# Row numbers of a feed-forward's dequantization constants: from VectorE in the first layer's attention to GpSimd at the front, and the pieces behind them one step earlier

## The chip, the core and the metric

The kernel runs on one core of one Trainium2 chip. The metric is the device time of one execution in microseconds (us). Before the change it is 2844.29 us, the median of three runs (2843.87 to 2844.41).

Engines are named as in the profile: PE is the TensorE matrix engine and PEld its weight load, DVE is VectorE, ACT is ScalarE, POOL is GpSimd, and SP is the engine whose queue issues most of the DMAs. L190 stands for line 190 of the kernel before.

## The reference

Two transformer layers run one after the other on 2048 tokens of width 512 (32 sequences of 64). Each layer is a cross-attention with 32 query heads and 8 key heads, followed by a feed-forward part. The second layer's feed-forward is a small memory lookup, which the change does not touch. The first layer's feed-forward has weights of 4 bits, which are unpacked with a scale and a zero for every group of 128 rows:

```python
x = x + _L0_xattn_ref(_layernorm(x), ctx_4096, ctx_4096, mask1, wq, wk, wv, wo)
x = x + _L0_ffn_ref(_layernorm(x), qweight_gu, qzeros_gu, scales_gu, g_idx_gu,
                    qweight_down, qzeros_down, scales_down, g_idx_down)
x = x + _L1_xattn_ref(_layernorm(x), ctx_4096, mask0, q_w, k_w, v_w, o_w, q_norm, k_norm)
x = x + _L1_ffn_ref(_layernorm(x), ...)

def _L0_ffn_ref(x, qweight_gu, qzeros_gu, scales_gu, g_idx_gu, ...):
    def _dequant(qw, qz, sc, g_idx):
        wq = (qw[:, None, :] >> shifts & 15)          # 4-bit weights
        zq = (qz[:, :, None] >> shifts & 15) + 1.0    # 4-bit zeros, one per group and column
        return sc[g_idx] * (wq - zq[g_idx])           # a row's group picks its scale and zero
    gate, up = split(x @ _dequant(gu))                # 512 -> 2 x 1376
    return (silu(gate) * up) @ _dequant(down)         # 1376 -> 512
```

## The kernel before

**Tiling.** The 2048 tokens are four chunks of 512. Attention runs over eight key heads g, each with its four query heads, and over the four chunks c: 32 steps (g, c), which this text numbers 4g + c, from step 0 to step 31. Each large product is cut into 2 x 2 blocks and made of seven block products where eight would be usual (`quarters` and `output_first`/`output_rest`); for that POOL adds and subtracts blocks of the operands (`left_sums`, `right_sums`).

**One step of the first layer's attention** (`Attention.run`, L672). While DVE, ACT and POOL work on the softmax of step i, PE finishes the output product of the step before (`output_rest`), projects the keys of step i+1 (`pk`, L375), projects its queries (`P`, L189, seven block products), multiplies probabilities and values (`po`, L609), projects the next values (`pv`, L407), begins the output product of step i (`O`, L189) and takes the next scores (`S`, L508). So the first `pk` of a step marks one step's beginning on PE, and the distance from one to the next is the length of a step. In a query projection ACT copies a block product out of PSUM (`h`, L214), DVE adds the next one to it (L439), ACT and DVE turn it by its position (`rotate`, L422 to L425) and POOL adds the two halves (L426). Keys are turned the same way (`rk`). In steps with c = 0 and g > 0, POOL has four more operations in this stretch, the `right_sums` of the output weights `wo` (L174 to L177), and in steps with c = 3 the `left_sums` of the next query weights.

**The order of the work.** The program is written as a list. A scheduler at build time orders the instructions of each engine: the order of the text is the priority, but an instruction that is ready in its model while earlier ones are not may be put ahead of them. `tc.issue_after(ins)` holds the instructions of a block on `ins`'s engine behind `ins`. On the chip each engine, and each DMA queue, then works strictly in that fixed order. Buffers of one tag go round: `tmp` has two of 128 x 1024 values (every `rotate` takes one), `m2` has four of 128 x 512 (the softmax takes two per step).

**The constants** (`ffn_constants`, L775) are made in pieces by a generator. In `att0.run` the argument `late` (L1350) takes one piece in each of the 24 steps 4 to 27, behind the last output addition on DVE (L709 to L711). The pieces are, in this order:

- one piece: the row numbers `pidx` (L781 to L795). Each of four ranges of partitions gets a counter from POOL (`iota`), and then DVE makes of it two flags, -1 where the counter has reached one or two times the number of groups, and takes that number off where a flag is set. That leaves group numbers in column 0 and the flags in columns 1 and 2.
- seven pieces: the scales, 512 columns at a time (L798 to L814). Three DMAs bring the columns into a `tmp` buffer, and five DVE operations split them into three bf16 parts, with the flags as a scalar operand.
- eight pieces: the zeros (L815 to L833). Two DMAs bring them into an `m2` buffer; each piece unpacks two of eight nibbles with four DVE operations.
- eight pieces: the group numbers (L834 to L856). One DMA each, and four DVE operations that compare with column 0 of `pidx`.

They are used from step 30 on, by the matmuls L922 and L940.

**The front.** Four DMAs on ACT's queue bring the first chunk of x. DVE takes its statistics (`norm_stats`, L258 to L262), POOL makes the reciprocal root (`rsqrt`, L247), DVE scales (L272), PE transposes (L286), ACT copies back (L290), and POOL makes the `right_sums` of the result. Before that POOL sets a few small constants (L117 to L147).

Of the kernel before, what the change touches and what calls it, by code (L numbers as in the profile page):

```python
# [9 lines left out]
F32 = mybir.dt.float32  # L10
BF16 = mybir.dt.bfloat16
# [4 lines left out]
ALU = mybir.AluOpType  # L16
AX = mybir.AxisListType

P = 128
# [14 lines left out]
INTER = 1376  # L34
# [10 lines left out]
def tile_xattn_ffn_2_layers(ctx: ExitStack, tc: tile.TileContext, a: dict, out: bass.AP):  # L45
    nc = tc.nc
# [5 lines left out]
    const = ctx.enter_context(tc.tile_pool(name="const", bufs=1))  # L52
# [12 lines left out]
    def m2_tile(name):  # L65
        return ap_.tile([P, CH], F32, tag="m2", name=name, bufs=4)
# [19 lines left out]
    def tmp_tile(name):  # L86
        return ap_.tile([P, 2, CH], F32, tag="tmp", name=name)
# [157 lines left out]
    def rsqrt(dst, src):  # L245

        return nc.gpsimd.tensor_tensor(dst, src, nhalf[:, : src.shape[-1]], ALU.pow).ins  # L247
# [3 lines left out]
    def norm_stats(c, name, at_once=TT):  # L251

        st = sm.tile([P, TT, 6], F32, tag="st", name=f"st{name}{c}")
        mv = sm.tile([P, TT, 2], F32, tag="mv", name=f"mv{name}{c}")
        ve = sm.tile([P, TT], F32, tag="ve", name=f"ve{name}{c}")
        rs = sm.tile([P, TT], F32, tag="rs", name=f"rs{name}{c}")
        for t in range(TT):
            nc.vector.bn_stats(st[:, t, :], x_sb[c][:, t, :])  # L258
            nc.vector.bn_aggr(mv[:, t, :], st[:, t, :])
            if (t + 1) % at_once == 0:  # L260
                part = slice(t + 1 - at_once, t + 1)
                nc.vector.tensor_scalar(ve[:, part], mv[:, part, 1], EPS, None, ALU.add)  # L262
                rsqrt(rs[:, part], ve[:, part])
        norms[c] = mv, rs
# [36 lines left out]
    def norm_apply(c, name):  # L301
        norm_scale(c, name)
        return norm_turn(c, name)
# [468 lines left out]
    NG, NGD = a["scales_gu"].shape[0], a["scales_down"].shape[0]  # L772
    ffn = {}

    def ffn_constants():  # L775


        both = const.tile([P, 3 * INTER], BF16, tag="c8", name="szoh")
        sz, oh = both[:, 0 : 2 * INTER], both[:, 2 * INTER :]
        pidx = const.tile([P, 3], F32, tag="pidx", name="pidx")  # L780
        for base, cnt, parts in ((R_GS, NG, 3), (R_GZ, NG, 1), (R_DS, NGD, 3), (R_DZ, NGD, 1)):  # L781
            rows = slice(base, base + parts * cnt)
            idx, p1, p2 = (pidx[rows, k : k + 1] for k in range(3))
            nc.gpsimd.iota(
                idx,
                pattern=[[0, 1]],
                base=0,
                channel_multiplier=1,
                allow_small_or_imprecise_dtypes=True,
            )  # L790

            nc.vector.tensor_scalar(p1, idx, float(cnt), -1.0, ALU.is_ge, ALU.mult)
            nc.vector.tensor_scalar(p2, idx, float(2 * cnt), -1.0, ALU.is_ge, ALU.mult)
            for p_ in (p1, p2):
                nc.vector.scalar_tensor_tensor(idx, p_, float(cnt), idx, ALU.mult, ALU.add)  # L795
        ffn["sz"], ffn["oh"] = sz, oh
        yield
        for base, cnt, name in ((R_GS, NG, "scales_gu"), (R_DS, NGD, "scales_down")):  # L798
            rows = slice(base, base + 3 * cnt)
            _, p1, p2 = (pidx[rows, k : k + 1] for k in range(3))  # L800
            total = a[name].shape[1]
            for at in range(0, total, CH):
                w = min(CH, total - at)
                s = tmp_tile(f"{name}{at}")
                v, part = s[rows, 0, 0:w], s[:, 1, :].bitcast(BF16)[rows, 0:w]
                for k in range(3):
                    nc.sync.dma_start(
                        s[base + k * cnt : base + (k + 1) * cnt, 0, 0:w], a[name][:, at : at + w]
                    )
                for by in (p1, p2):  # L810
                    nc.vector.tensor_copy(part, v)
                    nc.vector.scalar_tensor_tensor(v, part, by, v, ALU.mult, ALU.add)
                nc.vector.tensor_copy(sz[rows, at : at + w], v)
                yield  # L814
        qz = m2_tile("qz").bitcast(U32)  # L815
        zi = m2_tile("zi").bitcast(U32)
        for base, cnt, name in ((R_GZ, NG, "qzeros_gu"), (R_DZ, NGD, "qzeros_down")):
            w = a[name].shape[1]
            rows = slice(base, base + cnt)
            nc.sync.dma_start(qz[rows, 0:w], a[name])  # L820
            zv = sz[rows, 0 : 8 * w].rearrange("p (w e) -> p w e", e=8)
            for e in range(8):
                nc.vector.tensor_scalar(
                    zi[rows, 0:w],
                    qz[rows, 0:w],
                    4 * e,
                    15,
                    ALU.logical_shift_right,
                    ALU.bitwise_and,
                )  # L830
                nc.vector.tensor_copy(zv[:, :, e], zi[rows, 0:w])
                if e % 2 == 1:
                    yield  # L833
        for base, cnt, parts, name in (  # L834
            (R_GS, NG, 3, "g_idx_gu"),
            (R_GZ, NG, 1, "g_idx_gu"),
            (R_DS, NGD, 3, "g_idx_down"),
            (R_DZ, NGD, 1, "g_idx_down"),
        ):
            rows = slice(base, base + parts * cnt)  # L840
            total = a[name].shape[1]
            for at in range(0, total, CH):
                w = min(CH, total - at)
                gt = tmp_tile(f"{name}{base}_{at}")
                gv, o = gt[rows, 0, 0:w].bitcast(I32), gt[rows, 1, 0:w]
                nc.sync.dma_start(
                    gv, a[name][0:1, at : at + w].to_broadcast([parts * cnt, w])
                )

                nc.vector.tensor_scalar(o, gv, 0.0, float(cnt), ALU.is_lt, ALU.mult)  # L850
                nc.vector.tensor_tensor(o, o, gv, ALU.add)
                nc.vector.tensor_scalar(o, o, 0.0, float(cnt - 1), ALU.max, ALU.min)
                nc.vector.tensor_scalar(
                    oh[rows, at : at + w], o, pidx[rows, 0:1], None, ALU.is_equal
                )
                yield  # L856
# [457 lines left out]
    nc.sync.dma_start(wqk[:, 0:1], a["q_norm"])  # L1314
    nc.sync.dma_start(wqk[:, 1:2], a["k_norm"])

    norm_stats(0, "a")
    first = norm_apply(0, "a")
    att0.start()

    def behind_first(c):
        with tc.issue_after(first):
# [3 lines left out]
            if c < last:  # L1326
                load_mask(c + 1)
                norm_stats(c + 1, "a")
                norm_apply(c + 1, "a")

    pieces = ffn_constants()
    first_up = []

# [149 lines left out]
```

## Time and profile before

| what | us |
|---|---|
| median of the runs | 2844.29 |
| the profiled execution, its own time | 2844.26 |
| its span in the profile | 2842.5 |
| PE busy in the span | 2796.1 |
| DVE, POOL and ACT busy | 1874.9, 1322.1 and 835.1 |
| length of most steps of the first attention | 35.38 |
| step 4 (row numbers, c = 0) | 37.93 |
| step 8 (fifth piece of scales, c = 0) | 36.68 |
| step 12 (first piece of zeros, c = 0) | 37.32 |
| steps 16, 20 and 24 (c = 0) | 35.38, 36.16 and 35.94 |

The execution's own time is 1.8 us longer than its span, which runs from the first to the last instruction. Lengths of steps are distances between the starts of the first `pk` matmuls (190.67 and 228.60 us for step 4, for instance). In lines of the timeline the columns are: start and duration in us, engine, line, operation, output <- input, shapes and count (several like instructions in a row are merged into one line), and in brackets the idle time before with what ended it.

### The profile page before, as it was taken

To read this page: it belongs to the slowest core of one execution; us is meant where nothing else is said; L and a number is where in the kernel's file an instruction comes from. 1 tells how busy PE (TensorE), PEld (TensorE's weight loads), DVE (VectorE), ACT (ScalarE), POOL (GpSimd) and SP (SyncE) were. 2 spreads that over 40 slices of the span, in tenths; PEclk is the share of its full clock that TensorE was granted. 3 is DMA by queue.
4 is the path that set the end of the run, shared out by engine and by line. 5 is a ranking of instruction groups with operands and counts; after the bars stand their busy time and mean duration, and the time that the engine had idled before them with its cause. 6 is when DMAs were issued, how large, how long until landed. Compare 5 with 4: busy or idle time off the path is not lost. (4 is left out here: it accounts for less than half of the span.)

```text
span 2842.5 us, 41235 instructions
## 1 busy us (share of the span) xinstructions
PE 2796.1 (98%) x16742; PEld 2259.8 (80%) x16742; DVE 1874.9 (66%) x2805; ACT 835.1 (29%) x1415; POOL 1322.1 (47%) x1039
## 2 busy tenths in 40 slices
PE   7999999999999999999999999999999999999998
PEld 5878787888888887888888677888888888888775
DVE  7777777777777777756655665555555555555667
ACT  3333333333333333311111322222222222222244
POOL 5554545454545455644443444444444444444332
PEclk9999999999999999999999999999999999999999
DMA  4111111111111110100001102111111111111001
GB/s 165 34 52 45 54 42 57 36 62 38 60 39 61 38 60 16 53 23 23 23 6 37 48 30 62 43 53 45 53 45 53 45 52 45 53 45 53 30 1 60
DMA packets 103812, 130.77 MB, mean 46 GB/s; under 512 B 8725, under 2 KB 65165, under 8 KB 103623
## 3 DMA queue, kind: packets, MB, share of 16 engines
q1 hardware_dynamic: 103047, 127.09, 13.8%
q8 instruction: 133, 2.18, 0.3%
q10 hardware_dynamic: 576, 1.05, 0.1%
q14 instruction: 56, 0.46, 0.1%
HBM read 123.92 MB, written 4.19 MB: 45 GB/s over the span
## 5 line engine op out<-in xcount | busy, mean ns | idle before, releaser
L189 PE MATMUL O<-wo,oT 128*128 128x256 f32 x3584 | 802.3, 381 | 0.6 <-DVE x L242 0.5
L189 PE MATMUL P<-xnT,wq 128*128 128x256 f32 x3584 | 789.4, 380 | 10.6 <-ACT h L214 10.5
L189 PEld LDWEIGHTS P<-xnT,wq 128*128 128x128 f32 x3584 | 682.1, 191 | 133.7 <-issue 35.1
L189 PEld LDWEIGHTS O<-wo,oT 128*128 128x128 f32 x3584 | 670.3, 190 | 114.3 <-issue 24.6
L242 DVE TENSOR_TENSOR x<-x,O 128x512 f32<-128x512 f32 (+1 forms) x448 | 368.6, 823 | 235.7 <-PE O L189 235.5
L589 POOL TENSOR_TENSOR s<-s,ib 128x512 f32<-128x512 f32 x128 | 169.4, 1343 | 518.4 <-DVE ib L313 471.8
L214 ACT COPY h<-P 128x512 f32<-128x512 f32 (+1 forms) x352 | 202.4, 575 | 561.0 <-PE P L189 559.3
L247 POOL TENSOR_TENSOR qr<-qs,nhalf 128x20 f32<-128x20 f32 x32 | 113.4, 3543 | 382.7 <-DVE qs L496 382.7
L426 POOL TENSOR_TENSOR qT<-h,rq 128x512 f32<-128x512 f32 x128 | 175.4, 1370 | 237.6 <-DVE rq L425 237.6
L583 ACT ACTIVATE s<-s 128x1024 f32<-128x1024 f32 x64 | 67.7, 1057 | 735.9 <-DVE s L581 735.9
L189 PE MATMUL P<-xnT,wgu 128*128 128x256 f32 (+1 forms) x1232 | 271.3, 380 | 0.4 <-DVE x L242 0.2
L189 PEld LDWEIGHTS P<-xnT,wgu 128*128 128x128 f32 (+1 forms) x1232 | 229.8, 187 | 40.2 <-DVE x L242 4.3
L407 PE MATMUL pv<-wkv,ctxT 128*128 128x128 f32 x1984 | 246.2, 280 | 1.6 <-DVE h L439 1.6
L407 PEld LDWEIGHTS pv<-wkv,ctxT 128*128 128x128 f32 x1984 | 228.5, 192 | 23.0 <-issue 18.2
L375 PE MATMUL pk<-ctxT,wkv 128*128 128x512 f32 x496 | 223.2, 593 | 0.3 <-DVE h L439 0.3
L422 ACT COPY rq<-h 64x512 f32<-64x512 f32 x256 | 157.9, 617 | 124.1 <-DVE h L439 119.1
L424 DVE TENSOR_TENSOR h<-h,cosT 128x512 f32<-128x512 f32 x128 | 92.7, 724 | 123.8 <-ACT rq L422 123.6
L375 PEld LDWEIGHTS pk<-ctxT,wkv 128*128 128x128 f32 x496 | 94.1, 190 | 93.5 <-issue 89.6
L457 DVE TENSOR_TENSOR qT<-h,P 128x512 f32<-128x512 f32 x128 | 87.7, 686 | 100.8 <-PE P L189 94.3
L463 DVE TRANSPOSE_TENSOR_REDUCE part<-q 128x16 f32<-128x512 f32 x128 | 90.8, 709 | 87.6 <-ACT q L459 83.8
L965 DVE TENSOR_TENSOR h<-h,P 128x512 f32<-128x512 f32 (+1 forms) x96 | 61.1, 640 | 127.7 <-PE P L189 95.0
L972 POOL TENSOR_TENSOR hT<-h,h 128x512 f32<-128x512 f32 (+1 forms) x48 | 56.5, 1181 | 187.4 <-DVE h L965 187.4
(250 smaller groups left out, 3418.9 us busy)
## 6 DMA issues: line engine op xcount, KB each, us to landing
ctxT<-in_ctxT SPq DMA_DIRECT2D x62, 1024.0 KB
wq<-in_L_wq SPq DMA_DIRECT2D x32, 256.0 KB
wo<-in_L_wo SPq DMA_DIRECT2D x32, 256.0 KB
wq<-in_L_wqT SPq DMA_DIRECT2D x32, 256.0 KB
wo<-in_L_woT SPq DMA_DIRECT2D x32, 256.0 KB
wgu<-in_qweight_gu SPq DMA_DIRECT2D x40, 128.0 KB
out<-o SPq DMA_DIRECT2D x16, 256.0 KB
x<-in_x SPq DMA_DIRECT2D x12, 256.0 KB
```

Source lines behind the costliest of these rows:

```text
L189: ins = nc.tensor.matmul(pv[0:w, m, :], left[:, l, k, m * P : m * P + w], right[:, r, k, :], start=(first and m == 0 and k == 0), stop=(k ...
L214: last_copy = nc.scalar.copy(t[size], ps[size]).ins
L242: return nc.vector.tensor_tensor(dst, dst, src, ALU.add).ins
L247: return nc.gpsimd.tensor_tensor(dst, src, nhalf[:, : src.shape[-1]], ALU.pow).ins
L375: nc.tensor.matmul(ps, wkv[:, k, 0, :], ctxT[:, k, :], start=(k == 0), stop=(k == KT - 1))
L407: nc.tensor.matmul(ps[:, t * HD : (t + 1) * HD], ctxT[:, k, t * P : (t + 1) * P], wkv[:, k, 1, :], start=(k == 0), stop=(k == KT - 1),)
L422: nc.scalar.copy(t[lo:hi, 1], src[HD - hi : HD - lo])
L424: nc.vector.tensor_tensor(view(x), view(src), over(cosT), ALU.mult)
L426: nc.gpsimd.tensor_tensor(dst(None), dst(x), dst(t[:, 1]), ALU.add)
L457: nc.vector.tensor_tensor(q, xv, yv, ALU.add)
L463: nc.vector.tensor_reduce(part[:, i, f], q2.rearrange("p (g q) -> p g q", q=KB), AX.X, ALU.add, apply_transpose=True,)
L589: nc.gpsimd.tensor_tensor(sv[:, f], sv[:, f], ib[:, f * W : (f + 1) * W].unsqueeze(1).to_broadcast([P, KH, W]), ALU.mult,)
```

## The change

- The `iota`s and the arithmetic on `pidx` leave the generator. A new function `ffn_indices` does them, called at the front right ahead of `norm_stats(0, "a")`.
- The arithmetic goes from DVE to POOL. [...]
- The arithmetic is made for two of the four ranges only, those with three parts; the other two keep their counter. So 16 operations on DVE become 12 on POOL: eight `tensor_scalar` and four `tensor_tensor`. The four `iota`s stay.
- The generator loses its first `yield`. So the first piece of scales runs where the row numbers ran (step 4), each later piece runs one step sooner, and step 27 has none.

```diff
-    def ffn_constants():
-        both = const.tile([P, 3 * INTER], BF16, tag="c8", name="szoh")
-        sz, oh = both[:, 0 : 2 * INTER], both[:, 2 * INTER :]
-        pidx = const.tile([P, 3], F32, tag="pidx", name="pidx")
+    pidx = const.tile([P, 4], F32, tag="pidx", name="pidx")
+
+    def ffn_indices():
         for base, cnt, parts in ((R_GS, NG, 3), (R_GZ, NG, 1), (R_DS, NGD, 3), (R_DZ, NGD, 1)):
             rows = slice(base, base + parts * cnt)
             idx, p1, p2 = (pidx[rows, k : k + 1] for k in range(3))
             nc.gpsimd.iota(idx, ...)
-            nc.vector.tensor_scalar(p1, idx, float(cnt), -1.0, ALU.is_ge, ALU.mult)
-            nc.vector.tensor_scalar(p2, idx, float(2 * cnt), -1.0, ALU.is_ge, ALU.mult)
+            if parts == 1:
+                continue
+            tt, ts = nc.gpsimd.tensor_tensor, nc.gpsimd.tensor_scalar
+            ts(p1, idx, float(cnt), -1.0, ALU.is_ge, ALU.mult)
+            ts(p2, idx, float(2 * cnt), -1.0, ALU.is_ge, ALU.mult)
+            x = pidx[rows, 3:4]
             for p_ in (p1, p2):
-                nc.vector.scalar_tensor_tensor(idx, p_, float(cnt), idx, ALU.mult, ALU.add)
+                ts(x, p_, float(cnt), None, ALU.mult)
+                tt(idx, idx, x, ALU.add)
+
+    def ffn_constants():
+        both = const.tile([P, 3 * INTER], BF16, tag="c8", name="szoh")
+        sz, oh = both[:, 0 : 2 * INTER], both[:, 2 * INTER :]
         ffn["sz"], ffn["oh"] = sz, oh
-        yield
         for base, cnt, name in ((R_GS, NG, "scales_gu"), (R_DS, NGD, "scales_down")):
...
+    ffn_indices()
     norm_stats(0, "a")
     first = norm_apply(0, "a")
     att0.start()
```

## The prediction, made before the changed kernel was run

> **What bounds the kernel now.** I read the busy times first, then the waits of PE, then the lengths of the steps, then the step and the front that the change touches. PE is the bound:
>
> ```profile
> PE 2796.1 (98%) x16742; PEld 2259.8 (80%) x16742; DVE 1874.9 (66%) x2805; ACT 835.1 (29%) x1415; POOL 1322.1 (47%) x1039
> ```
>
> It is not busy for 2842.5 - 2796.1 = 46.4 us, so work on DVE or POOL counts only where it makes PE wait. The view of PE's waits (who waited for whom: total us, times, longest us) says where:
>
> ```profile
> PE xta L286 <- DVE xna L272: 12.0, 2, 11.8
> PE P L189 <- ACT h L214: 10.5, 7, 3.2
> ...
> PE pv L407 <- DVE h L439: 1.6, 4, 0.6
> ```
>
> 11.8 us is the start, before the first transpose. The second and fourth lines are query projections in which DVE is late with the addition L439: a block buffer comes free late, ACT copies late, PE waits. PE's timeline gives the place of one of them, and the lengths of steps:
>
> ```profile
> 190.67 3.60 PE L375 MATMUL pk<-ctxT,wkv 128*128 128x512 f32 x8
> 205.19 3.72 PE L189 MATMUL P<-xnT,wq 128*128 128x256 f32 x16 [2.29 <-ACT h L214]
> 228.60 3.60 PE L375 MATMUL pk<-ctxT,wkv 128*128 128x512 f32 x8
> 263.98 3.60 PE L375 MATMUL pk<-ctxT,wkv 128*128 128x512 f32 x8
> ```
>
> 263.98 - 228.60 = 35.38 us is an undisturbed step, 228.60 - 190.67 = 37.93 is step 4. All steps from 4 to 27 are 35.38 except 4 (+2.55), 8 (+1.30), 11 (+0.11), 12 (+1.94), 20 (+0.78) and 24 (+0.56): 7.24 us is all that pieces of constants can cost now. Five of the six have c = 0, where POOL also makes the sums of `wo`. Step 4's timeline on DVE and POOL shows why:
>
> ```profile
> 193.51 0.10 DVE L795 SCALAR_TENSOR_TENSOR pidx<-pidx 12x1 f32<-12x1 f32 x1
> ...
> 193.75 2.49 POOL L589 TENSOR_TENSOR s<-s,ib 128x512 f32<-128x512 f32 x2 [10.71 <-DVE pidx L795]
> 193.88 1.15 DVE L795 SCALAR_TENSOR_TENSOR pidx<-pidx 12x1 f32<-12x1 f32 x1
> ...
> 197.88 3.40 DVE L795 SCALAR_TENSOR_TENSOR pidx<-pidx 30x1 f32<-30x1 f32 x3
> ...
> 202.51 0.68 DVE L439 TENSOR_TENSOR h<-h,P 128x512 f32<-128x512 f32 x1
> ```
>
> A dozen values take 0.10 us while POOL is idle and 1.15 while it runs a large addition: DVE waits for POOL's operation to end, and each short instruction pays that anew. The 16 operations hold DVE from 192.75 to 201.28, so L439 comes 202.51 - 190.67 = 11.84 us into the step. Taking PE's resumption minus its wait in steps 4, 8 and 12 (14.52 - 2.29, 12.65 - 0.43, 13.90 - 1.67) gives 12.22 to 12.23 each time, so L439 has until about 11.84 - 2.29 = 9.6 us.
>
> The Trainium skill, page "GPSIMD Engine Reference", its opening table: GpSimd's SBUF interfaces are shared with VectorE, with contention for VectorE instructions that have two SBUF inputs or run in a two-port mode. The pair 0.10 and 1.15 agrees.
>
> **Step 4: row numbers out, scales in.** Out go 16 DVE operations, in come the five of a scales piece (two casts, two multiply-adds, one last cast). The same piece at the same kind of step is step 8's: there its operations stand between 336.81 and 342.90, and the keys' L424 starts 342.83 - 334.74 = 8.09 us into the step; in step 4 it starts 201.31 - 190.67 = 10.64. I take step 8's length whole: 36.68 - 37.93 = **-1.25**. Bounds: -2.55 (nothing left) and 0 (POOL's order holds DVE as long). Still late there is step 8's own remainder, 0.43 on `P` and 0.30 on `pv`. Its three DMAs go ahead of a load of ctx and the four of `wo` on SP's queue; in step 8 these are issued at 320.12, 321.12 and 334.93, the last held by PE and not by the three, which cost SP 0.95 us. The buffer they need comes free at the last turned query of the step before, as there. So 0 for the DMAs; without the 14 us between, a `wo` would land 1 us later.
>
> **Step 12: zeros, first piece out, second in.** Now DVE waits 0.54 us for the zeros' DMA (issued at 478.84 between loads of `wo`), the piece runs from 481.33 to 487.44 through POOL's sums, and L439 comes 11.23 us in. The second piece has no DMA. In step 13 it ends 521.73 - 514.99 = 6.74 us in, with its reciprocal (L586) at 1.33; with c = 0 that stands at 1.91 (step 8), so the piece ends near 7.3. L424 at 6.36 (step 20) went with a length of 36.16, at 8.09 (step 8) with 36.68; on that line 7.3 gives 36.44: **-0.88**. Bounds: -1.94 and 0. The wait for the DMA moves to step 11, c = 3, in which no `wo` is loaded and SP's queue is free after 429.7 + 0.5 until 463.7. There L439 stands at 9.46 behind the scales of 5.05 us (444.93 to 449.98), and the zeros take about as long: 0, at most +0.5.
>
> **The other pieces.** Step 16 gets the second pair of a set for the first, like for like (both 0.19, 0.31, 1.12 and 1.31 us): 0. Step 20 gets 4 x 512 for 12 x 512 (800.74 to 805.43 against 764.71 to 769.07, 0.33 longer), step 24 gets 10 x 512 for 30 x 352 (942.80 to 947.52 against 907.12 to 911.40, 0.44 longer). By the slope of the two steps above (0.52 per 1.73 us) that is +0.10 and +0.13, or +0.22 for step 24 if it becomes step 20: together **+0.3**, bounds 0 and +0.6. Step 8 keeps a piece of the same shape: 0. All steps with c = 1 to 3 but step 11 are 35.38 with pieces of each kind, cover included: 0. Step 27 loses a piece that cost nothing. `tmp` and `m2` are taken as often as before, one step sooner; the constants are used 100 us later.
>
> **The front.** POOL gets four `iota`s and twelve small operations ahead of the `rsqrt` that starts the whole chain; behind it wait the scaling, the transposes and PE.
>
> ```profile
> 9.81 0.17 DVE L262 TENSOR_SCALAR vea<-mva 128x4 f32<-128x4 f32 x1
> ...
> 10.14 1.07 POOL L247 TENSOR_TENSOR rsa<-vea,nhalf 128x4 f32<-128x4 f32 x1 [8.60 <-DVE vea L262]
> ...
> 11.18 1.09 POOL L784 IOTA pidx<- 12x1 f32 x4
> ```
>
> POOL is idle for 8.60 us there, from 1.54. No row shows these operations on one column; nearest are groups of 128 x 4 (busy us, mean ns):
>
> ```profile
> L1126 POOL TENSOR_SCALAR up<-rsd 128x4 f32<-128x4 f32 x4 | 2.1, 533 | 0.3
> L1127 POOL TENSOR_TENSOR up<-mvd,rsd 128x4 f32<-128x4 f32 x4 | 1.4, 354 | 0.0
> L1128 POOL TENSOR_SCALAR up<-up 128x4 f32<-128x4 f32 x4 | 1.4, 352 | 0.3
> L1265 POOL TENSOR_SCALAR g_ub<-g_lv,g_rec 128x4 f32<-128x4 f32 x1 | 0.7, 725 | 0.0
> L1267 POOL TENSOR_SCALAR g_ub<-g_ub 128x4 f32<-128x4 f32 x1 | 0.7, 674 | 0.7 <-DVE g_ub L1266 0.7
> ```
>
> Back to back the first three take 1.04 us together (2679.59 to 2680.63), 0.35 each; the five from L1267 to L1271 take 2.41 (2832.74 to 2835.15), 0.48 each. 1.54 + 1.09 + 12 x 0.48 = 8.4 us, 1.7 before POOL is needed: **0**. With the longest, 0.725, it is 11.3: +1.2. With the farthest row, the 1.03 us of a `rsqrt` of 128 x 4, 15.0: +4.9. No gain is possible: the chain waits for x until 8.87. What is late on this chain passes to PE whole, which has no gap from the transposes to `P` at 22.73. On DVE an early POOL operation could hold a statistic by one small operation; idle time of 0.5 to 0.9 us ahead of each covers that.
>
> The Trainium skill, same page, section "Elementwise — side-by-side cycle accounting", speaks against the move: elementwise work belongs on VectorE while GpSimd's software is as it is. By that each operation should be dearer on POOL, and 0.35 against 0.10 agrees; it changes nothing while the 8.60 us cover it.
>
> **Sum.** -1.25 - 0.88 + 0.3 + 0 = -1.8 us. On the profiled execution: span 2840.7, own time 2842.4; that run was 0.03 below the median, so **2842.5**. The bounds add to -4.5 (-2.55 - 1.94) and +2.3 (0.6 + 0.5 + 1.2), for 2839.8 and 2846.6.
>
> **Rivals.** 0.2% or 5.7 us is taken as what a measurement here tells from no change.
>
> 1. *The wait is refilled.* POOL's sums of `wo` pace DVE in steps 4 and 12 whatever stands there. For it: step 8 has 1.30 left with five operations. Against: its wait is 0.43 against 2.29. 2844.3 us; 12%.
> 2. *The front becomes the bound, slower than before.* The twelve operations outlast the 8.60 us; from (8.60 - 1.09) / 12 = 0.63 us each on, PE starts later by all that is over, from 0.78 on (1.8 us over) the gain is gone. At 1.03 each: -1.8 + 4.9, 2847.4 us. For it: single rows of 0.53 to 0.73. Against: rows in sequence of 0.35 and 0.48. 10%, 2 of them over +5.7. The Trainium skill (same page, section "Instruction dispatch") has about 6 us for the first call of a freshly loaded GpSimd kernel; by that too PE would start some 4 us late. POOL's first `tensor_scalar` before (L1126, 2679.59) stands 0.1 us behind the operation ahead of it and takes 0.53, so the trace does not bear it out.
> 3. *The change does not put the work where it says.* The scheduler may leave the operations behind the `rsqrt`, as it placed the `iota`s at 11.18 though POOL was idle. Then 1.09 + 5.8 us fall into the 5.4 until the `right_sums` at 16.66, 1.5 too much, of which 1.0 is spare (they end at 21.74, `P` starts at 22.73): +0.5 - 1.8, 2843.0 us; 5%.
> 4. *The new order helps beyond its place.* All six excesses go, 7.2 us: 2837.1. For it: DVE's order is chosen anew in each step. Against: steps 8, 20 and 24 keep their kinds. 9%.
> 5. *The new order hurts.* Two waits like the longest single ones now (3.2 us on `P` and 3.2 on `S`) appear: 2850 us or more. For it: step 0 already has such crowding. Against: each piece has run beside each kind of step without one. 9%.
>
> **The chances.** The forecast has 55%, the rivals 12, 10, 5, 9 and 9. Faster by over 0.2%: 0.09 (rival 4). Slower: 0.09 + 0.02 = 0.11. Within: 0.80. The range that leaves out rivals 4, 5 and the end of 2 is the sum's lower bound with a little room, 2839.0, to rival 2's 2847.5. The likeliest case alone has 2839.8 to 2844.
>
> **What would show it.** Right: `P` of step 4 waits under 1 us, steps 4 and 12 are near 36.7 and 36.4, all of `ffn_indices` is over before the first `rsqrt`, and that starts at 10.1. Wrong: the first transpose after 11.85; a wait of `pv` or `P` in steps 5 to 11; PE waiting for a DMA of ctx or `wo`.

## The result and the profile after

| | before | after |
|---|---|---|
| median of 22 runs each (us) | 2845.42 (2843.55 to 2847.68) | 2840.56 (2838.89 to 2842.22) |
| the profiled execution, its own time | 2844.26 | 2839.60 |
| its span | 2842.5 | 2837.8 |

The ratio is 0.9983 with a 95% interval of 0.9978 to 0.9989: the change gains 4.9 us, 0.17%, where 1.8 us was predicted. The busy times first:

```profile
PE 2795.7 (99%) x16742; PEld 2260.1 (80%) x16742; DVE 1868.5 (66%) x2789; ACT 834.8 (29%) x1415; POOL 1329.7 (47%) x1051
```

PE does the same work in the same time (2796.1 before). DVE has 16 instructions less and 6.4 us less, POOL twelve more and 7.6 us more; by itself neither says anything of the end. PE's waits do (what PE waited for: total us, times, longest):

```profile
PE xta L286 <- DVE xna L272: 12.2, 1, 12.2
PE P L189 <- ACT h L214: 7.0, 6, 3.2
...
PE pv L407 <- DVE h L439: 1.5, 4, 0.6
```

The waits on the query projection fell from 10.5 us in seven to 7.0 in six. Step 4 on PE, to be laid beside the four lines of before:

```profile
190.88 3.60 PE L375 MATMUL pk<-ctxT,wkv 128*128 128x512 f32 x8
...
203.55 3.72 PE L189 MATMUL P<-xnT,wq 128*128 128x256 f32 x16 [0.43 <-ACT h L214]
...
209.50 3.84 PE L407 MATMUL pv<-wkv,ctxT 128*128 128x128 f32 x32 [0.29 <-DVE h L439]
...
227.57 3.60 PE L375 MATMUL pk<-ctxT,wkv 128*128 128x512 f32 x8
```

The 2.29 us wait is 0.43, with 0.29 on `pv`: the pair that step 8 had before. The step is 227.57 - 190.88 = 36.69 us. All lengths of steps, read in the same way:

| step | before | predicted | after | difference |
|---|---|---|---|---|
| 4 | 37.93 | 36.68 | 36.69 | -1.24 |
| 8 | 36.68 | 36.68 | 36.68 | 0 |
| 11 | 35.49 | 35.49 | 35.38 | -0.11 |
| 12 | 37.32 | 36.44 | 36.01 | -1.31 |
| 20 | 36.16 | 36.26 | 35.60 | -0.56 |
| 24 | 35.94 | 36.07 to 36.16 | 35.63 | -0.31 |
| others of 4 to 27 | 35.38 | 35.38 | 35.38 | 0 |

That is -3.53 us. The rest of the 4.7 us between the two spans is, to within 0.2, +0.2 at the front (the first `pk` of step 4 starts at 190.88 instead of 190.67) and -1.49 in step 32, the first of the second layer's attention, which the change does not touch: 44.80 us became 43.31. PE has the same wait there in both, and takes unequally long behind it. Before, then after:

```profile
1634.47 6.63 PE L189 MATMUL P<-xnT,wq 128*128 128x256 f32 x16 [3.22 <-ACT h L214]
```

```profile
1631.06 5.13 PE L189 MATMUL P<-xnT,wq 128*128 128x256 f32 x16 [3.21 <-ACT h L214]
```

Sixteen matmuls that take 3.72 us in step 4 take 6.63 and 5.13. The windows of before around that place (start and end; the length, then busy us of PE, PEld, DVE, ACT and POOL with counts; the granted clock; DMA share and GB/s) show the clock at half speed behind the wait:

```profile
1634.00:1636.00 2.00, 1.52 (x4) 1.29 (x5) 1.97 (x5) 0.33 (x1) 0.00 (x0) 0.50 0.00 0
1636.00:1638.00 2.00, 2.00 (x6) 1.57 (x5) 1.76 (x4) 0.63 (x1) 1.15 (x1) 0.50 0.01 4
```

Eleven profiled executions of eight kernels, four of them of the kernel before, have step 32 at 42.91 (twice), 43.31 to 43.56 (five) and 44.80 to 44.93 (four), with the kernel before among the middle and the long ones. The clock records of the traces go with it: no half clock in step 32 in the two shortest, 3.41 us of it in the five, 6.83 us in the four. So this 1.5 us belongs to the execution and not to the change.

At the front the order on POOL is not the one forecast:

```profile
1.49 0.65 POOL L782 IOTA pidx<- 12x1 f32 x4
10.48 1.07 POOL L247 TENSOR_TENSOR rsa<-vea,nhalf 128x4 f32<-128x4 f32 x1 [8.34 <-DVE vea L262]
11.63 0.53 POOL L793 TENSOR_SCALAR pidx<-pidx 12x1 f32<-12x1 f32 x1
...
16.80 0.44 POOL L798 TENSOR_TENSOR pidx<-pidx 12x1 f32<-12x1 f32 x2
17.32 1.27 POOL L174 TENSOR_TENSOR xnT<-xnT 128x512 f32<-128x512 f32 x1
```

The four `iota`s moved into the idle time, the twelve operations did not: they fill 11.63 to 17.25, behind the `rsqrt`, and the `right_sums` start at 17.32 instead of 16.66. They end at 22.40, still ahead of `P`, which starts at 22.95, when PE is done with `pv` (19.38 to 23.11 as modelled). `P` starts 0.22 later than before, and ahead of it the first transpose 0.33 later (12.18) and the `rsqrt` 0.34 (10.48), since the last statistic of x starts at 9.21 instead of 8.87. The twelve operations, which come later, cannot have caused that; in three further profiles of the kernel before, the first transpose starts at 11.79, 11.90 and 12.08, and in the experiment "No piece beside the sums where none fits", whose kernel has the front of after, at 11.95.

Step 12 shows where the wait for the DMA went. DVE in after, with what is left of the piece of zeros; in before L823, the first of these operations, started at 481.33 behind 0.54 us for its DMA, and L439 came 11.23 us into the step:

```profile
478.84 0.33 DVE L831 TENSOR_SCALAR zi<-qz 4x344 uint32<-4x344 uint32 x1
...
482.07 1.88 DVE L839 CAST szoh<-zi 4x344 bf16<-4x344 uint32 x1
483.99 0.69 DVE L424 TENSOR_TENSOR rk<-pk,cosT 128x512 f32<-128x512 f32 x1
...
485.41 0.67 DVE L439 TENSOR_TENSOR h<-h,P 128x512 f32<-128x512 f32 x1
```

The step begins at 476.52, so L439 stands at 8.89, before the 9.6 that the prediction allowed; PE no longer waits on `P` there, and 0.32 on `pv`; the other half of the 0.63 by which the step is longer than 35.38 passes mostly within its `O` matmuls, without a wait of over 0.1 us. The zeros' two DMAs are issued at 428.75 and 429.14, at the end of a row of loads, and nothing waits for them.

### The profile page after: what moved, and what is told of

It is laid out like the page before. It is cut to its first block, busy times and chain, and to the rows that moved or that the text cites. A ratio compares the mean times of both kernels' runs of the same rounds, so it can differ in the third digit from the quotient of the medians.

```text
span 2837.8 us, 41231 instructions
## 1 busy us (share of the span) xinstructions
PE 2795.7 (99%) x16742; PEld 2260.1 (80%) x16742; DVE 1868.5 (66%) x2789; ACT 834.8 (29%) x1415; POOL 1329.7 (47%) x1051
## 5 line engine op out<-in xcount | busy, mean ns | idle before, releaser
L424 DVE TENSOR_TENSOR h<-h,cosT 128x512 f32<-128x512 f32 x128 | 91.1, 712 | 125.6 <-ACT rq L422 125.4
```

The lines of the kernel that those rows point to most:

```text
L424: nc.vector.tensor_tensor(view(x), view(src), over(cosT), ALU.mult)
```

## The experiments

The letters in the expectations: A is the prediction's account, in which each part acts in the step where its work stands; B is the rival to it; C is the clock, by which a long wait of PE costs more than its own length in some executions. Where they say e4, the experiment "Small pieces beside the sums" is meant; f1 is the first repeat of the kernel before. All kernels but the three repeats of the one before were timed beside the kernel before, and each ratio is to its runs on the same chip.

**The row numbers moved, the pieces not.** The kernel after, with the first `yield` back, so that step 4 has no piece at all:

```diff
         ffn["sz"], ffn["oh"] = sz, oh
+        yield
```

> The row numbers go to GpSimd at the front as in the change, but their place in the list of pieces stays empty, so every other piece runs in the step where it ran before. Theory A (each part works in its own step): step 4 falls from 37.93 to 35.38 us, steps 8, 12, 20 and 24 stay at 36.68, 37.32, 36.16 and 35.94; 2.6 us less than before by the step lengths. Rival B (it is the shift of the other pieces that brings the gain): step 4 keeps a wait, and the time is within 1 us of before. Rival C (a wait of over 2 us also lowers TensorE's clock in many executions, which no single profile of before shows): the median falls by 1.5 us more than the step lengths do, 4 us in all.

Median 2842.26 (2839.22 to 2844.93, 11 runs) against 2846.32, ratio 0.9985 (0.9977 to 0.9994). Step 4 is 35.38, steps 8, 11, 12, 20 and 24 have before's lengths to within 0.02, and only step 28 rose (+0.24). So the row numbers cost step 4's whole excess of 2.55 and act nowhere else among steps 5 to 27: A holds for the steps, and B falls. The steps give 2.3 us and the median fell by 4.1, which is the figure of C; the interval, 1.7 to 6.5 us, holds both, so the time does not decide on C.

**The pieces moved, the row numbers not.** The kernel before, without the `yield`: row numbers on DVE and the first scales, both in step 4.

```diff
         ffn["sz"], ffn["oh"] = sz, oh
-        yield
```

> The row numbers stay on VectorE in step 4, but the other pieces run one step sooner, so step 4 has both the row numbers and the first piece of scales. Theory A: steps 12, 20 and 24 are as after the change (36.01, 35.60 and 35.63, together 2.2 us less than before), step 4 is longer by the 5.4 us that the scales hold VectorE, near 43.3 us; in all about 3.2 us more than before. Rival B (the shift alone brings the gain): step 4 within 1 us of before, the time 2 us under it. Rival C (a long wait lowers the clock): behind the wait of 7 to 8 us in step 4 the granted clock falls to a half for at least 3 us, and step 4 is 45 us or more.

2846.09 (2845.47 to 2848.36, 11 runs) against 2846.32, ratio 1.0002 (0.9993 to 1.0011). Steps 12, 20 and 24 are 35.89, 35.62 and 35.61, after's to within 0.13: the gain of these three belongs to the shift of the pieces alone. B falls: step 4 is 43.35, very near A's figure, but not for A's reason. PE, then DVE:

```profile
207.55 6.62 PE L189 MATMUL P<-xnT,wq 128*128 128x256 f32 x16 [4.80 <-ACT h L214]
```

```profile
201.33 0.74 DVE L811 SCALAR_TENSOR_TENSOR scales_gu<-scales_gu,pidx 12x512 f32<-12x512 bf16 x1
202.10 0.16 DVE L795 SCALAR_TENSOR_TENSOR pidx<-pidx 10x1 f32<-10x1 f32 x1
```

The wait is 4.80 us, not 7 to 8, because POOL's sums end at 201.27 and what is late on DVE then runs at its own speed, 0.74 and 0.16 us. The other 2.9 us are the sixteen matmuls behind it, 6.62 us instead of 3.72, at half clock:

```profile
206.00:208.00 2.00, 0.45 (x1) 0.45 (x2) 1.08 (x2) 1.46 (x3) 0.42 (x1) 0.66 0.00 0
208.00:210.00 2.00, 2.00 (x6) 1.55 (x6) 0.81 (x2) 1.09 (x2) 1.27 (x1) 0.50 0.00 0
```

Two errors cancelled in A's figure for the step. C's mechanism is seen in the step that the change is about, the half clock lasting 6.83 us, though the 45 us that C asked for, with its longer wait, were not reached. In time A missed: it asked for 3.2 us more than before, and the median is 0.2 less. The steps of this profile, of an execution of 2847.38, do give +3.1, of which 2.9 are the half clock. That the other executions, down to 2845.47, have less of it would explain the median, but only this one was profiled.

**The row numbers at the front, on DVE.** The kernel after, with before's sixteen DVE operations in `ffn_indices`:

```diff
-            if parts == 1:
-                continue
-            tt, ts = nc.gpsimd.tensor_tensor, nc.gpsimd.tensor_scalar
-            ts(p1, idx, float(cnt), -1.0, ALU.is_ge, ALU.mult)
...
+            nc.vector.tensor_scalar(p1, idx, float(cnt), -1.0, ALU.is_ge, ALU.mult)
+            nc.vector.tensor_scalar(p2, idx, float(2 * cnt), -1.0, ALU.is_ge, ALU.mult)
             for p_ in (p1, p2):
-                ts(x, p_, float(cnt), None, ALU.mult)
-                tt(idx, idx, x, ALU.add)
+                nc.vector.scalar_tensor_tensor(idx, p_, float(cnt), idx, ALU.mult, ALU.add)
```

> As after the change, but the 16 operations on the row numbers stay on VectorE and run at the front, behind the first statistics and ahead of the first scaling. Theory A (what counts is that they leave step 4; the engine counts only through the front): all steps as after, the first transpose later by what 16 operations of about 0.1 us take beyond the 0.57 us in which VectorE waits for the reciprocal root: about 1 us later than after, so 1840 plus 1000, that is 2841.5 us or about 3.8 us under before. Rival (the engine makes no difference at all): the first transpose at 12.2 us and the time equal to after. Rival (GpSimd's operations of the front delay VectorE's short ones to 1 us each as in step 4): the first transpose 8 us later, slower than before.

(Where this says "1840 plus 1000", 2840.6 plus 1 is meant.) 2842.50 (2840.94 to 2843.07, 11 runs) against 2846.32, ratio 0.9987 (0.9979 to 0.9996). Steps 4 to 27 are after's to within 0.13. The eight L795 of before are here L793 (in the view of one tile: durations in ns as least, median and greatest; first and last start):

```profile
L793 DVE SCALAR_TENSOR_TENSOR pidx<-pidx x8: 148/150/156, 11.2 to 13.2; 12x1 f32<-12x1 f32 x2, 4x1 f32<-4x1 f32 x2, 30x1 f32<-30x1 f32 x2, 10x1 f32<-10x1 f32 x2
```

In step 4 of before the same eight had 104, 992 and 1201 ns. So DVE is not slow at them; the time went to standing beside POOL's sums. But here they stand in front of the scaling that PE waits for:

```profile
10.71 0.14 DVE L790 TENSOR_SCALAR pidx<-pidx 12x1 f32<-12x1 f32 x1
...
13.34 1.46 DVE L272 TENSOR_SCALAR xna<-x,mva,rsa 128x512 f32<-128x512 f32 x3
```

L272 starts at 13.34, against 11.24 in before and 11.58 in after, and the first transpose at 13.94 against 11.85 and 12.18: some 2 us are lost, about twice what was expected. By this the first rival, that the engine makes no difference at the front, falls, and so does the second (8 us later). The median's gain, 3.8 us, is A's figure, but its interval (1.1 to 6.0) also holds the 4.9 of after.

**The row numbers one step earlier, on DVE.** The kernel before, with the list begun in step 3 (c = 3, no sums of `wo`); every piece is one step sooner, as in after, and GpSimd keeps only its `iota`s:

```diff
-        late={(g, c): [lambda: next(pieces, None)] for g in range(1, NKV - 1) for c in range(NCH)},
+        late={
+            (g, c): [lambda: next(pieces, None)]
+            for g in range(NKV - 1)
+            for c in range(NCH)
+            if g > 0 or c == NCH - 1
+        },
```

> The kernel before with its whole list of pieces one step earlier: the row numbers stay 16 operations on VectorE, but run in step 3 (c = 3), where GpSimd makes no sums of wo; all other pieces as after the change. Theory A (the price of the row numbers comes from standing beside GpSimd's sums): in step 3 only the operations beside the 2.5 us of the probabilities' product are held, the others take 0.1 to 0.15 us, the step stays at 35.38, all others are as after (36.69, 36.68, 36.01, 35.60, 35.63), and the time is that of after, about 4.5 us under before. Rival (16 short instructions cost VectorE 8 us wherever they stand): step 3 is 37 us or more, and the gain is 2 us or less. Rival (the engine matters: GpSimd at the front was needed): anywhere slower than after by over 1 us.

2840.57 (2839.17 to 2842.24, 11 runs) against 2844.97, ratio 0.9986 (0.9976 to 0.9995). Step 3 is 35.38, undisturbed, and steps 4, 8, 11, 12, 20 and 24 are 36.68, 36.68, 35.38, 35.88, 35.59 and 35.61: after's, to within 0.13. On DVE one sees why step 3 bears what step 4 did not:

```profile
160.59 1.15 DVE L795 SCALAR_TENSOR_TENSOR pidx<-pidx 12x1 f32<-12x1 f32 x1
...
161.94 1.03 DVE L795 SCALAR_TENSOR_TENSOR pidx<-pidx 4x1 f32<-4x1 f32 x1
...
163.90 0.53 DVE L795 SCALAR_TENSOR_TENSOR pidx<-pidx 30x1 f32<-30x1 f32 x3
```

While POOL's two softmax additions run (160.47 to 162.96) one L795 takes 1.15 or 1.03; after them three take 0.53 together, where step 4 of before had 3.40. Both rivals fall. The whole gain of the change is had without moving an instruction to GpSimd.

**Small pieces beside the sums.** The kernel after, its pieces taken by a plan, in which `s` is a piece of scales, `u` of zeros of gate and up (4 x 344), `d` of zeros of down (10 x 64) and `g` of group numbers; a row is steps 4 to 7, 8 to 11 and so on:

```diff
...
+        plan = (
+            d, u, u, u,
+            d, u, s, s,
+            d, s, s, s,
+            d, s, s, g,
+            None, g, g, g,
+            g, g, g, g,
+        )
+        for piece in plan:
+            if piece is not None:
+                next(piece)
+            yield
```

The lines left out make one generator of each kind of piece.

> The change plus another order of the pieces: the four smallest ones (the zeros of the down projection, 2.9 us of VectorE) run in steps 4, 8, 12 and 16, none in step 20, one group-number piece in step 24, and all other pieces in steps in which GpSimd does not make the sums of wo. Theory A (only the steps with those sums have no room): steps 4, 8, 12, 16 and 20 at 35.38, step 24 at 35.63, all others at 35.38; 3.5 us less than after, about 8 us less than before (ratio 0.9972). Rival (the room goes elsewhere: the other steps are as tight once the long pieces of zeros meet the left sums): some step with c = 1 to 3 grows by 0.3 to 2 us, and the time is within 1 us of after.

2838.85 (2837.6 to 2840.15, 8 runs) against 2846.32, ratio 0.9973 (0.9963 to 0.9983). Steps 8, 12, 16 and 20 are 35.37 to 35.38, and so are all with c = 1 to 3, so the rival falls; 24, with a piece of group numbers, is 35.95 where 35.63 was expected. Step 4 is 35.93 and not 35.38, with its zeros landing late:

```profile
195.75 0.62 DVE L838 TENSOR_SCALAR zi<-qz 10x64 uint32<-10x64 uint32 x1 [0.87 <-DMA qz<-in_qzeros_down]
```

**No piece beside the sums where none fits.** The same with the plan below, whose first row is step 3 alone and whose next is steps 4 to 7; `late` begins in step 3:

```diff
...
+        plan = (
+            s,
+            None, u, u, u,
+            d, u, s, s,
+            d, s, s, s,
+            d, s, g, g,
+            d, g, g, g,
+            None, g, g, g,
+        )
...
```

> As e4, with one piece of scales in step 3 and none in steps 4 and 24; steps 8, 12, 16 and 20 have the four smallest pieces. Theory A: steps 3 to 27 are all 35.38 us; by the lengths 1.1 us less than e4 and 3.7 us less than after, near 2837 us (ratio to before about 0.997). Rival (step 3, in which the first layer's masks are still made, has no room): step 3 grows by 0.5 to 2 us and eats the gain.

2836.77 (2835.01 to 2837.24, 6 runs) against 2844.74, ratio 0.9969 (0.9957 to 0.9981): the best version, 0.3% under before and below every run of after. Its interval still touches that of after (0.9978 to 0.9989); the lengths of the steps tell the two apart. All steps from 3 to 27 are 35.37 to 35.40, so the rival falls, and of the waits on `P` only 5.1 us are left (same view as above):

```profile
PE P L189 <- ACT h L214: 5.1, 4, 3.2
```

**The kernel before, three times more,** to see whether the clock falls behind step 4's wait. Nothing is edited.

> The kernel before, unchanged, for another profiled execution. Theory A (only the lengths of the steps): step 4 is 37.93 and step 12 is 37.32, as in the first profile, in every execution. Rival C (the clock): in executions of over 2845.5 us the granted clock falls to a half behind the wait of 2.29 us in step 4 or of 1.67 us in step 12, and that step is 1.5 to 3 us longer.

> As f1, a third execution. Theory A: steps 4 and 12 at 37.93 and 37.32. Rival C: one of them 1.5 to 3 us longer with the clock at a half, where the execution is over 2845.5 us.

> As f1, a fourth execution. Theory A: steps 4 and 12 at 37.93 and 37.32. Rival C: one of them 1.5 to 3 us longer with the clock at a half, where the execution is over 2845.5 us.

One profiled execution each: 2846.54, 2844.38 and 2844.11 us. Step 12 is 37.31, 37.32 and 37.32; step 4 is 39.62, 37.94 and 37.93. The first of them:

```profile
207.00 5.41 PE L189 MATMUL P<-xnT,wq 128*128 128x256 f32 x16 [2.29 <-ACT h L214]
```

The wait is the same 2.29 us as ever, and the matmuls behind it take 5.41 instead of 3.72, at a granted clock of 0.50 from 208 to 210. So in one of four profiled executions of the kernel before, and the only one of over 2845.5, step 4 cost 1.69 more than in the others, as C asked. Step 12's wait of 1.67 was not followed by it in any of the four. Step 0, behind its 3.2 us wait on `S`, is 47.17, 46.11 and 45.75 in the three.

## Why the prediction was right or wrong

**The time.** 2842.5 was forecast with a range of 2839.0 to 2847.5, and "within 0.2%" at 80%; 2840.56 lies in the range and the gain of 0.17% in that class. The sum of the steps was -1.8, the profile has -3.53 for the same terms, and the step that failed is the pieces', as follows. The number was met with some luck: before came out at 2845.42 this time and not at 2844.29, from which the same gain gives 2839.4, below the sum's own bound of 2839.8; and the interval of the gain reaches 0.22%, outside the class.

**Step 4, -1.25.** Measured -1.24. Taking the length whole from a step with the same piece and the same sums was right to 0.01 us, down to the waits of 0.43 and 0.29. Its DMAs cost nothing, as said. The index-only run gives the parts: -2.55 for the row numbers taken out, +1.31 for the scales put in. One reading behind it was too wide: not each of the 16 short instructions waits for POOL. The eight L795, which read `pidx` twice, do; the eight L792 and L793 took 0.08 to 0.15 us each, beside the sums too (0.14 at 195.04 and at 196.29). No term of the sum rests on that.

**Step 12, -0.88.** Measured -1.31; right in its mechanism, mis-sized. L424 was put "near 7.3" us in and came at 483.99 - 476.52 = 7.47. The slope between steps 20 and 8 was wrong: it joined two steps whose DVE meets POOL's sums at other moments, and it predicts 36.5 for 7.47 where 36.01 came out. The limit of 9.6 for L439, worked out in the same text, would have told without a slope that no wait on `P` is left: it came at 8.89. (The limit is borne out by the run with only the pieces moved: L439 at 14.42 went with a wait of 4.80, 9.62 again.) It says nothing of the 0.63 that stayed. That the zeros' DMA, moved to step 11, would cost nothing there held: step 11 even lost its 0.11.

**"The other pieces", +0.3.** Measured -0.87 for steps 20 and 24, and -0.98 with step 11. Here the sign was wrong. The step of the argument that failed is that a piece 0.33 us longer makes its step longer by the slope. The pieces were longer, as forecast (the first 762.37 to 767.06 against 764.71 to 769.07), and the first query's L424 behind them, in step 20 of before and then of after, shows what decided:

```profile
773.33 1.27 POOL L177 TENSOR_TENSOR wo<-wo 128x512 f32<-128x512 f32 x1
773.34 1.81 DVE L424 TENSOR_TENSOR h<-h,cosT 128x512 f32<-128x512 f32 x1 [1.73 <-ACT rq L422]
```

```profile
769.83 1.27 POOL L176 TENSOR_TENSOR wo<-wo 128x512 f32<-128x512 f32 x1
770.88 0.76 DVE L424 TENSOR_TENSOR h<-h,cosT 128x512 f32<-128x512 f32 x1 [1.54 <-ACT rq L422]
```

In before POOL's fourth sum begins at 773.33, in the same moment as L424, which takes 1.81. In after L424 begins inside the third, which ends at 771.10, and gets through in 0.76 us. With that, `pv`'s wait of 0.47 in before is gone. L424 itself stands 10.70 us into the step both times; POOL's sums moved. The step begins at 762.64 in before and at 760.18 in after, so the fourth sum begins 10.69 in, then 10.87: with the longer piece, L313, which POOL's softmax additions wait for, ends 3.34 us in instead of 3.04. A third of a microsecond more work on DVE put its neighbour later, and the meeting of the two cost a microsecond less. That these lengths come with the shift of the pieces and not with the row numbers is shown (the runs with one of the two alone); that this one instruction is the whole cause in step 20 is read from the trace and not tested, and step 24 was not traced.

**The front, 0.** Right in its price and wrong in its place. That all of `ffn_indices` would be over before the first `rsqrt` is refuted, and rival 3, which had 5% and +0.5 us, is what happened to the twelve operations, not to the `iota`s: the order made at build time left them behind the `rsqrt`. They took 5.62 us, 0.47 each, against the 0.48 taken from the nearest rows; the spare time ahead of `P` swallowed the delay, so its price was 0. The first transpose did start after 11.85, the sign named for "wrong", but by x's arrival. Rival 2 (POOL at 1.03 each) falls by the measured 0.47, and with it the fear from the Trainium skill's page "GPSIMD Engine Reference", section "Instruction dispatch": the first of these operations took 0.53 us, not 6.

**The other rivals.** Rival 1 (the wait is refilled) falls: step 4 without a piece has no wait on `P` at all, though POOL's sums are there. Rival 4 named the right kind of thing, a better order beyond the moved work, in a smaller dose: 0.98 of gain in steps 11, 20 and 24, where it asked for all six excesses. Rival 5 falls; the only new waits in steps 4 to 27 are the two of 0.3 on `pv`, in steps 4 and 12, in place of longer ones on `P`.

**What was not in the sum at all: the clock.** The prediction costed a wait at its own length. Step 4's wait of 2.29 us was followed by half clock in one of four executions, and cost 1.69 us more there. Removing the wait removes that too. The median gained 4.9 us (by the interval 3.1 to 6.3), the steps give 3.5, and 1.69 in a quarter of the executions would give 0.4 more on average. The runs hint that the remaining 1.0 is the clock too, oftener than four profiles show it. The mean granted clock was recorded for 55 runs of the kernel before, beside the experiments: 22 have 0.995 or 0.996, the others 0.997, while all 22 of after have 0.997 or 0.998. On the chip with 30 of these, the median is 2846.75 of the 15 runs with the lower clock and 2844.50 of the others. In the comparison with after, the 22 runs of before fall into eleven up to 2845.07 and eleven from 2845.77 on; the lower eleven have a median of 2844.29, 3.7 above after, which is what the steps give. Behind which wait the clock fell in these runs is not known: the index-only kernel, with no wait in step 4, has 0.996 in 5 of its 11.

## What to carry to other kernels

The stall here came from two engines in each other's way, and it was mended by where a piece stands, not by which engine does it: one step earlier on the same engine gave the same time as moving it to GpSimd, and a plan that keeps every long piece out of the crowded steps gave the most. Price a moved piece by a step that has the same piece and the same neighbours, or else by the latest start of the instruction that releases the bound engine; a line through two other steps can miss the sign. And count a long wait of the matrix engine at more than its length, since the clock may fall behind it.

## What the runs showed of the hardware

- **Short DVE operations wait out POOL's.** The same eight operations on one column took a median of 150 ns with POOL idle, 992 beside its sums in step 4, and 154 in step 3, where POOL has only the softmax additions. Not all short ones do: `tensor_scalar` on one column took 0.08 to 0.15 us in step 4 too, while that on 10 x 64 uint32 took 0.19 with POOL idle (at 623.33 in before) and 1.12 beside the softmax additions (at 624.64). What sets the two apart was not tested. The Trainium skill, page "SBUF — State Buffer", section "Terms", describes the port pair of the two engines as locked by one instruction for its whole length, with the other fully blocked; the 1.15 us beside additions of 1.25 us agree. Small POOL operations cost DVE little: beside the twelve at the front DVE's L166 to L169 took 0.69 us each, as before.
- **Waits of 2.3 to 4.8 us, then half clock, or not.** 2.29 us was followed by a granted clock of 0.50 in one of four executions; 3.2 us in step 32 cost nothing more in two of eleven, some 0.5 in five and some 1.9 in four; the 3.2 us in step 0 were followed by half clock in six of eleven; 4.80 us in the one profile that has it cost 2.9. In these three steps the half clock lasts 3.41 or 6.83 us each time. The Trainium skill, page "TensorE: Matmul & The Clock Gate", section "HAM oscillation — how this bites in real kernels", puts the limit at gaps of over 3.4 us; the 2.29 us here were enough once and the 3.2 us of step 32 nine times of eleven, so for this kernel the limit is too high. Its explanation, a window of activity that runs free of the program (Part 1 of the page), fits that the same wait is answered differently from one execution to the next.
